# Two metaformer layers on one core: small VectorE work moved to GpSimd, one fetch per tile for the small Mamba, new durations and places in the planner

## The chip, the cores and the metric

The kernel runs on one core of a Trainium2 chip. The metric is the device time of one execution in microseconds (us). A core has TensorE (PE, with its weight loads PEld), VectorE (DVE), ScalarE (ACT), GpSimd (POOL) and SyncE (SP), each with its own list of instructions that it works off in order, and 16 DMA engines. Nearly all DMAs are issued by SP, the indirect ones (gathers and scatters of rows) by POOL.

## The reference

The input `x` is 8 images of 256 channels and 32 x 32 positions (1024 tokens). Two layers follow each other. In short:

```python
# layer 0
x = x + mamba0(ln_c(x))            # 512 inner channels, 16 states, 1024 steps in time:
                                   # h = exp(dt*A)*h + dt*xs*B ;  y = sum_s h*C + xs*D ; y*silu(z)
t = tokens(x)
t = t + moe(ln_t(t))               # 8 experts, top 2 of the softmax of the gate, gelu, hidden 512
# layer 1
x = x + conv1(ln_c(x))             # channels 0..127 kept; 3x3, 1x11 and 11x1 depthwise taps on 32 each;
                                   # a small mamba on the last 32 (64 inner channels, 16 states)
t = t + mod(ln_t(t))               # the best 511 of 1024 tokens pass a 256-1024-256 feed forward
```

`dt` is `softplus(...)`. Both Mambas are first-order recurrences along the tokens, one for each channel and state.

## The kernel before

The work is cut into 16 units (image, half of the 1024 tokens; `N = 512`) for the large Mamba, and 4 groups of two images for all that follows. A unit holds 512 channels as four tiles of 128; `scan_unit` goes over them in two couples `cp`, over the 16 states in 8 steps `sp` of two states `j`, and over the two tiles `n` of the couple. Each innermost step is one `scan_pair`:

- GpSimd multiplies `dtx` by a row of B for both states (L780, 128 x 1024, tile `dbu`),
- ScalarE makes `exp(dt*A)` into PSUM (L785), VectorE scans it with `dbu` (L788, `tensor_tensor_scan`) and multiplies by a row of C (L793), for each of the two states,
- TensorE adds the two products into `y` with an identity matrix (L804); where `paired` says so, GpSimd adds the two first (L797) and TensorE adds one. `PAIRED` gives, for each of the 16 units and the 4 small Mambas, in how many of 8 steps that is so.

The rows of B and C lie in DRAM (`rows`) and are spread over the partitions by DMA into tiles `bc` of 128 x 2 x 512 f32 (512 KB, four of them). The large Mamba fetches one tile by one DMA (L839, source `[128 (stride 0), 2 x 512]`), and two scan pairs share a couple of tiles. The small Mamba (`mamba_scan`, one for each group) has two images on the partitions, 64 each, whose rows differ, so a tile is fetched by two DMAs of 64 partitions (L1416), and each scan pair needs tiles of its own: 16 pairs and 32 tiles in each of the four scans.

`delta` makes `dt` (softplus as max(v, 0) + ln(1 + exp(-|v|))): TensorE product, ScalarE abs, exp and ln, VectorE max and sum (L758), and GpSimd's product `dtx = dt * xs` (L760). `small_rstd` makes `rstd` on ScalarE and `shift = -mean * rstd` on VectorE (L859), for tokens (128 x 4) and in `combine` (128 x 2). `gate` in `tokens` makes the gate's logits with four small VectorE operations (L914 to L917).

After four units, a group passes `route` (ranks of experts, VectorE), `scatter` (rows to their experts' slots), `experts` (23 blocks of 256 rows, weights fetched for each), `combine` (rows of the two experts of a token gathered by POOL, weighted and summed by TensorE with diagonal matrices `wdiag`, L1254 to L1263, evicted by ScalarE, L1267), `taps_of` (the convolutions on VectorE, L1323), `mamba_in`, `mamba_scan`, `mamba_out`, `assemble`, `ranks`, `feed_forward` and `finish`.

No engine's order is written by hand. Every step is declared with an engine, an estimated duration, a priority, and what it reads and writes; `Flow.run` is a list scheduler at build time that plays the steps against these estimates and emits them in the order in which it would start them. `PLAN` and `UNIT_AT` give the priorities ("places") of the stages; `dma` estimates a transfer at 2.3 us + KB / 180 behind its issue. Idle TensorE time in the plan is filled with dummy products (L525, L529). The estimates do not run on the chip: they decide only the order of each engine's list.

Of the kernel before, what the change touches and what calls it, by code (L numbers as in the profile page):

```python
# [30 lines left out]
AF = mybir.ActivationFunctionType  # L31
# [24 lines left out]

PAIRED = [2, 4, 0, 4, 3, 4, 7, 5, 5, 6, 8, 7, 5, 8, 6, 6, 7, 7, 5, 6]

# [3 lines left out]
PLAN = [  # L62
    dict(put=10.59, experts=(180, 8.0), combine=(355, 4.88), taps=(436, 2.05), mamba=464, assemble=(486, 1.12), ranks=500, ffn=(521, 4.8), finish=(570, 2.4)),
    dict(put=6.24, experts=(357, 6.25), combine=(465, 1.5), taps=(550, 0.75), mamba=541, assemble=(568, 2.41), ranks=628, ffn=(722, 4.8), finish=(767, 3.75)),
    dict(put=5.3, experts=(465, 5), combine=(602, 2.94), taps=(701, 1.84), mamba=666, assemble=(681, 1.88), ranks=699, ffn=(791, 2.81), finish=(827, 2.89)),
    dict(put=2.65, experts=(603, 4), combine=(692, 0.86), taps=(761, 0.77), mamba=775, assemble=(796, 0.43), ranks=795, ffn=(836, 3), finish=(873, 3.07)),
]
# [28 lines left out]
ENGINES = (PE, ACT, DVE, POOL, SP)  # L96
HOP = 0.08
SWITCH = 1.3
PACE = 1.07
AHEAD = 100  # L100
# [72 lines left out]
class Flow:  # L173
# [29 lines left out]
    def dma(self, prio, kb, run, reads=(), writes=(), fills=(), claims=(), us=0.4):  # L203
        return self.step(SP, us, prio, run, reads, writes, fills, claims, lat=2.3 + kb / 180)

    def run(self):
# [17 lines left out]
        def earliest(s):  # L224
            at = now[s.engine]
            for d in s.needs:
                at = max(at, d.end + (HOP if d.engine != s.engine or d.lat else 0.0))
            taken = {}
            for b in s.fresh:
                if b.v is None:  # L230
                    k = taken[b.pool] = taken.get(b.pool, 0) + 1
                    if not b.pool.has(k, b):
                        return None
                    at = max(at, sorted(b.pool.free)[k - 1][0] + HOP)
            if s.engine == SP and len(flying) >= QUEUE:
                at = max(at, sorted(flying)[-QUEUE])
            return at
# [61 lines left out]
def layers(g, ctx, x, a, out):  # L299
# [446 lines left out]

    def delta(parts, dts, dtxs, xs, prio):

        v, l = banks(2), buf("sq")
        for n in range(2):  # L750
            left, right, made = parts[n]
            step(PE, 0.9, prio, lambda n=n, left=left, right=right: nc.tensor.matmul(
                v[n].v, left, right(), start=True, stop=True), [made], [v[n]], claims=[*v, l, dts])
            step(ACT, 0.6, prio + 0.5, lambda n=n: nc.scalar.activation(l.v[:, n * N : (n + 1) * N], v[n].v, AF.Abs), [v[n]], fills=[l])
        step(ACT, 1.1, prio + 1, lambda: nc.scalar.activation(l.v, l.v, AF.Exp, scale=-1.0), [], [l], table="exp")
        step(ACT, 1.15, prio + 1, lambda: nc.scalar.activation(l.v, l.v, AF.Ln, bias=g.one), [], [l], table="exp")
        for n in range(2):
            step(DVE, 0.72, prio + 1.5, lambda n=n: nc.vector.scalar_tensor_tensor(  # L758
                dts.v[:, n], v[n].v, 0.0, l.v[:, n * N : (n + 1) * N], ALU.max, ALU.add), [v[n], l], fills=[dts])
        gpsimd(2.4, prio + 2, lambda: nc.gpsimd.tensor_tensor(dtxs.v, dts.v, xs.v, ALU.mult), [dts, xs], [dtxs])  # L760

    def dt_of(i, cp, prio):
        u = units[i]
        dts, dtxs = u[f"dt{cp}"], u[f"dtx{cp}"] = buf(f"dt{cp}"), buf(f"dtx{cp}")
        dbl = u["dbl"]
        parts = [
            (w_dt[: DR0 + 1, c * P : (c + 1) * P], lambda: dbl.v[: DR0 + 1], dbl) for c in (2 * cp, 2 * cp + 1)
        ]
        delta(parts, dts, dtxs, u[f"xs{cp}"], prio)

# [83 lines left out]
    def small_rstd(mv, rstd, shift, eps, prio, made, fill):  # L854

        step(ACT, 0.5, prio, lambda: (
            nc.scalar.activation(rstd(), mv()[:, :, 1:2], AF.Ln, bias=eps),
            nc.scalar.activation(rstd(), rstd(), AF.Exp, scale=-0.5)), made, fills=fill[:1], table="exp")
        return step(DVE, 0.6, prio, lambda: nc.vector.scalar_tensor_tensor(  # L859
            shift(), mv()[:, :, 0:1], -1.0, rstd(), ALU.mult, ALU.mult), [*made, fill[0]], fills=fill[1:])  # L860

    def tokens(i, prio):
# [47 lines left out]
        def gate():  # L910

            lg = grp["logits"].v[:, blks]
            wide = [P, nb, E]
            nc.vector.tensor_tensor(raw.v, raw.v, grp["rstd"].v[:, blks].to_broadcast(wide), ALU.mult)  # L914
            nc.vector.tensor_tensor(lg, gsum.to_broadcast(wide), grp["shift"].v[:, blks].to_broadcast(wide), ALU.mult)
            nc.vector.tensor_tensor(lg, lg, raw.v, ALU.add)
            nc.vector.tensor_tensor(lg, lg, gate_b.unsqueeze(1).to_broadcast(wide), ALU.add)  # L917

        step(DVE, 1.6, now, gate, [grp["rstd"], grp["shift"]], [raw], [grp["logits"]])

    def route(n, prio):
# [120 lines left out]
        for part in range(8):  # L1044
            step(DVE, 1.7, prio + 1 + 0.25 * part, lambda part=part: better(part), [lg], [r])
        step(DVE, 0.6, prio + 3, masks, [], [r])
        step(PE, 0.5, prio + 3, counts, [r], [pt])
        step(DVE, 1.0, prio + 3.5, sums, [pt], [r])
        step(DVE, 0.8, prio + 4, ends, [], [r])
# [8 lines left out]
    def put(kind, dest, slots, index, src, grp, prio, name, sources):  # L1058
# [20 lines left out]

        step(POOL, 1.15, prio, run, sources, fills=[slots], lat=2.5)  # L1080

# [148 lines left out]
    def combine(n, prio, each):  # L1230
# [6 lines left out]
        for m in range(NI):  # L1237
# [5 lines left out]
                xc.v, grp["gx"].v[:, at : at + 2]), [grp["gx"], grp["y"]], [xc], claims=[at_a, at_b]).opens = line  # L1243
            (t,), xo = banks(), buf("xo")
            for h in range(2):
                blk = i * NI + j + h
                ys, ds = buf("ys", line), buf("wdiag", line)
                for q in range(2):
# [3 lines left out]
                        in_offset=bass.IndirectOffsetOnAxis(ap=idx.v[:, blk : blk + 1], axis=0)),  # L1252
                        [grp["y"], idx], fills=[ys], lat=2.5)
                    step(ACT, 0.4, now - 1, lambda q=q, ds=ds, wt=wt, blk=blk: nc.scalar.activation(  # L1254
                        ds.v[:, q], g.ident, AF.Copy, scale=wt.v[:, blk]), [wt], fills=[ds])

                def product(h=h, blk=blk, ys=ys, ds=ds, xc=xc, t=t):
                    rows = slice(32 * (blk // 4), 32 * (blk // 4) + 32)
                    at = t.v[:, h * C : (h + 1) * C]
                    nc.tensor.matmul(at, g.ident, xc.v[:, h], start=True, stop=False)  # L1260
                    for q in range(2):
                        nc.tensor.matmul(at, ds.v[:, q], ys.v[:, q], start=False, stop=False)  # L1262
                    nc.tensor.matmul(at, grp["cwt"].v[rows], b2[rows, blk % 4], start=False, stop=True)  # L1263

                step(PE, 1.9, now, product, [ys, ds, xc, grp["cwt"]], [t], claims=[xo])
            bn = buf("bn")
            step(ACT, 0.6, now + 0.3, lambda xo=xo, t=t: nc.scalar.copy(  # L1267
                xo.v, t.v.rearrange("p (h c) -> p h c", h=2)), [t], [xo])
            dma(now + 0.5, 256, lambda xo=xo, two=two, i=i: nc.sync.dma_start(x1.v[:, two, i], xo.v), [xo], fills=[x1])
# [134 lines left out]
    def mamba_scan(n, pos):  # L1404
# [3 lines left out]
        for sp in range(DS // 2):  # L1408
            for hf in range(2):
                both = buf("bc"), buf("bc")  # L1410
                for j in range(2):

                    def fetch(j=j, hf=hf, sp=sp, both=both):
                        for i in range(2):
                            at = i * 2 * DS + j * DS + 2 * sp
                            nc.sync.dma_start(  # L1416
                                both[j].v[i * DI1 : (i + 1) * DI1],
                                grp["rows"][hf].v[at : at + 2].partition_broadcast(DI1),
                            )

                    dma(pos + 2 * sp + hf - 6, 512, fetch, [grp["rows"][hf]], [both[j]], us=0.8)
                scan_pair(
# [22 lines left out]
    def assemble(n, prio, each):  # L1445
# [8 lines left out]
        for j in range(NI):  # L1454
# [33 lines left out]

            step(DVE, 1.9, now + 0.7, stats, [xc], [bn, junk], [tok])

# [117 lines left out]
    def finish(n, prio, each):  # L1608
# [3 lines left out]
        for m in range(NI):  # L1612
# [6 lines left out]
            for h in range(2):  # L1619
# [3 lines left out]
                    in_offset=bass.IndirectOffsetOnAxis(ap=slot.v[:, 1, at : at + 1], axis=0)),  # L1623
                    [grp["y2"][i], slot], fills=[ys], lat=2.5)
                step(ACT, 0.59, now - 1, lambda h=h, at=at, xc=xc: nc.scalar.activation(
# [14 lines left out]

            step(DVE, 1.3, now, added, [tok, ys], [xc])
            step(PE, 0.7, now + 0.2, turned, [xc], [t], claims=[xo])
# [195 lines left out]
```

## Time and profile before

| | us |
|---|---|
| three runs, median (lowest to highest) | 3852.95 (3839.76 to 3853.16) |
| the profiled execution: time | 3870.05 |
| the profiled execution: span from first to last instruction | 3868.2 |
| large Mamba's scans, first to last (L788) | 58 to 2995 |
| small Mambas' scans of groups 2 and 3 | 3279 to 3386, 3558 to 3652 |
| busy: PE / DVE / ACT / POOL | 3299 / 2978 / 2207 / 2328 |

The profile is of one execution. Busy times are sums of instruction durations on an engine; a wait is idle time of an engine together with what ended it. A busy PE includes the dummy products. A line number names a line of the kernel. Lines such as `L1416 SPq DMA_DIRECT2D bc<-rows` are DMA issues: SP hands the transfer over and goes on, and the transfer lands later.

### The profile page before, as it was taken

The numbers are of one execution on the slowest core, as the hardware profiler recorded it, in microseconds if no ns is written. First come the engines' busy times: TensorE is split into PE (matmuls) and PEld (weight loads), VectorE is DVE, ScalarE is ACT, GpSimd is POOL, SyncE is SP. The second block draws the span as 40 slices with busy tenths as digits, with TensorE's granted clock in tenths as the row PEclk, the third lists the DMA queues.
The fourth block names the chain that finished last, engine by engine and source line by source line (L and its number), as shares of the span: only waits on it lengthen the run. The fifth ranks groups of instructions, "written<-read, shape, count | busy, mean of one in ns | idle before, by whom it ended". The sixth has DMA issues, their size and how long they took to land. (4 is left out here: it accounts for less than half of the span.)

```text
span 3868.2 us, 38209 instructions
## 1 busy us (share of the span) xinstructions
PE 3299.0 (85%) x10818; PEld 1849.4 (48%) x10818; DVE 2978.3 (77%) x4281; ACT 2207.2 (57%) x4010; POOL 2327.8 (60%) x1587
## 2 busy tenths in 40 slices
PE   8888888788889888978997798988987889799768
PEld 3333333333544444434553444554555666566446
DVE  4899899989679978976898898779787527557751
ACT  4555565465757557645765665665764456556433
POOL 3567567588577768866775886545765433424522
PEclk9999999999999999998999999999888989899989
DMA  6333333344544435535553558654669666967955
GB/s 232 122 123 131 114 131 132 106 151 162 200 139 167 165 129 194 181 111 172 172 174 122 195 181 226 204 184 136 200 204 223 222 213 214 243 215 215 247 175 168
DMA packets 277073, 676.67 MB, mean 175 GB/s; under 512 B 33063, under 2 KB 114349, under 8 KB 276862
## 3 DMA queue, kind: packets, MB, share of 16 engines
q1 hardware_dynamic: 258430, 623.88, 51.2%
q0 software_dynamic: 18432, 50.36, 4.1%
q8 instruction: 87, 1.43, 0.2%
q14 instruction: 124, 1.02, 0.1%
HBM read 572.92 MB, written 101.19 MB: 174 GB/s over the span
## 5 line engine op out<-in xcount | busy, mean ns | idle before, releaser
L780 POOL TENSOR_TENSOR dbu<-dtx,bc 128x1024 f32<-128x1024 f32 x576 | 1359.3, 2368 | 515.6 <-PE y L804 349.0
L804 PE MATMUL y<-dbu,ident 128*128 128x512 f32 x1564 | 822.6, 635 | 217.9 <-POOL dbu L797 185.7
L785 ACT ACTIVATE mm<-dt,neg_a 128x512 f32<-128x512 f32 x1152 | 770.3, 688 | 208.2 <-DVE dbu L793 190.4
L788 DVE TENSOR_TENSOR_SCAN mm<-mm,dbu 128x512 f32<-128x512 f32 x576 | 703.9, 1222 | 229.7 <-ACT mm L785 153.8
L793 DVE TENSOR_TENSOR dbu<-mm,bc 128x512 f32<-128x512 f32 x1152 | 796.4, 691 | 81.4 <-DMA bc<-rows 18.0
L788 DVE TENSOR_TENSOR_SCAN mm<-mm,state,dbu 128x512 f32<-128x512 f32 x576 | 738.2, 1282 | 59.5 <-POOL dbu L780 38.7
L797 POOL TENSOR_TENSOR dbu<-dbu 128x512 f32<-128x512 f32 x370 | 480.9, 1301 | 299.4 <-DVE dbu L793 291.3
L804 PEld LDWEIGHTS y<-dbu,ident 128*128 128x128 f32 x1564 | 281.6, 197 | 560.5 <-POOL dbu L797 278.7
L1179 PE MATMUL mm<-we,hid 128*128 128x256 f32 x1984 | 486.4, 398 | 36.0 <-ACT state L792 13.0
L792 ACT COPY state<-mm 128x1 f32<-128x1 f32 x576 | 91.4, 160 | 731.6 <-DVE dbu L793 710.9
L1157 PE MATMUL mm<-xbt,we 128*128 128x256 f32 x1984 | 474.3, 391 | 30.4 <-DMA we<-in_W12f 10.4
L1179 PEld LDWEIGHTS mm<-we,hid 128*128 128x128 f32 x1984 | 387.8, 199 | 156.3 <-issue 47.4
L1157 PEld LDWEIGHTS mm<-xbt,we 128*128 128x128 f32 x1984 | 383.4, 196 | 139.2 <-issue 46.9
L525 PE MATMUL y<-still 128*128 128x512 bf16 x1059 | 275.7, 395 | 0.0
L721 PE MATMUL mm<-pre,w_tap 128*128 128x512 f32 (+3 forms) x512 | 240.8, 612 | 28.6 <-ACT pre L708 27.3
L440 ACT ACT_TABLE_LOAD x176 | 225.8, 1283 | 3.1
L1250 POOL DMA_INDIRECT ys<-slots_y,slot x128 | 122.2, 954 | 160.0 <-PE mm L1262 69.0
L1163 ACT ACTIVATE hid<-mm,we 128x256 f32<-128x256 f32 x496 | 196.8, 475 | 37.8 <-PE mm L1157 29.1
L525 PEld LDWEIGHTS <-still 128*128 128x128 bf16 x1059 | 105.9, 101 | 192.6 <-issue 118.8
L721 PEld LDWEIGHTS mm<-pre,w_tap 128*128 128x128 f32 x512 | 95.5, 193 | 166.8 <-issue 103.9
L1068 POOL DMA_INDIRECT slots_x<-xg,slot x128 | 129.8, 1014 | 68.4 <-DVE acc_b L1323 31.2
L1621 POOL DMA_INDIRECT ys<-y,slot_t x64 | 63.1, 986 | 158.7 <-DVE xc L1631 59.0
(251 smaller groups left out, 3983.6 us busy)
## 6 DMA issues: line engine op xcount, KB each, us to landing
bc<-rows SPq DMA_DIRECT2D x512, 512.0 KB
bc<-rows SPq DMA_DIRECT2D x256, 256.0 KB
we<-in_W SPq DMA_DIRECT2D x92, 514.0 KB
we<-in_W SPq DMA_DIRECT2D x92, 512.0 KB
xb<-slots_x SPq DMA_DIRECT2D x92, 256.0 KB
slots_y<-xo SPq DMA_DIRECT2D x92, 256.0 KB
we<-in_W12f SPq DMA_DIRECT2D x32, 514.0 KB
xc<-x SPq DMA_DIRECT2D x64, 256.0 KB
```

Of the source, the lines that this page charges most:

```text
L440: nc.scalar.preload_act_table_set(tables[name])
L525: nc.tensor.matmul(live[0].v[:, 0], still, wide, start=False, stop=False)
L721: nc.tensor.matmul(tc_.v[:, cut:], w_tap[:, c, j], pre.v[:, cut + j : j + N], start=j == 3, stop=j == 0)
L780: gpsimd(2.45, prio, lambda: nc.gpsimd.tensor_tensor(dbu.v, dtxs.v[:, n : n + 1].to_broadcast(wide2), bt.v, ALU.mult), [dtxs, bt], [dbu], ...
L785: step(ACT, 0.69, prio, lambda j=j, h=h: nc.scalar.activation(h.v, dts.v[:, n], AF.Exp, scale=scales(j)), [dts], [h], table="exp", scan=True)
L788: step(DVE, 1.25, prio, lambda j=j, h=h: nc.vector.tensor_tensor_scan(h.v, h.v, dbu.v[:, j], 0.0 if initial is None else initial[1](j), AL ...
L793: step(DVE, 0.68, prio, lambda j=j, h=h: nc.vector.tensor_tensor(dbu.v[:, j], h.v, ct.v[:, j], ALU.mult), [h, ct], [dbu], scan=True)
L797: gpsimd(1.3, prio + 2.3, lambda: nc.gpsimd.tensor_tensor(dbu.v[:, 0], dbu.v[:, 0], dbu.v[:, 1], ALU.add), [], [dbu])
L804: nc.tensor.matmul(y.v[:, n], g.ident, dbu.v[:, j], start=False, stop=stop and (paired or j == 1))
L1157: nc.tensor.matmul(tv[:, f], we[0].v[:, at : at + P], xbt.v[:, k], start=k == 0, stop=k == KC - 1)
L1163: nc.scalar.activation(hid.v[:, f], tv[:, f % 2], func, bias=we[0].v[:, at : at + 1])
L1179: nc.tensor.matmul(to, hid.v[:, f, h * P : (h + 1) * P], we[1].v[:, f * C : (f + 1) * C], start=extra is None and f == 0, stop=f == FC - 1,)
```

## The change

The change does the following.

- `mamba_scan`: one DMA for each tile instead of two. Its source is a view of `rows` as `[2, 64 (stride 0), 2, 512]`, its destination the whole tile of 128 partitions.
- `delta`: except for unit 0, ScalarE writes `relu(v)` into `dts` (two instructions), and GpSimd adds `ln(1 + exp(-|v|))` (128 x 1024); VectorE's two operations are left out there.
- `small_rstd` and `gate`: the VectorE operations become GpSimd operations (two for `shift`, four for the gate).
- `combine` of groups 2 and 3: TensorE makes only the bias product (L1263); VectorE weights and adds the two experts' rows (two operations on each of two blocks) and adds `xc`; no `wdiag`, no eviction by ScalarE.
- `PAIRED`: 348 sums on GpSimd instead of 370, the others on TensorE.
- Planner: DMA estimate 3.4 us + KB / 250, indirect DMAs 3.0 to 3.3 us instead of 2.5, a `DRAIN` of 0.15 us behind TensorE, `PACE` 1.05 instead of 1.07, some step durations, and new places in `PLAN`.

The diff, cut to its core:

```diff
-PAIRED = [2, 4, 0, 4, 3, 4, 7, 5, 5, 6, 8, 7, 5, 8, 6, 6, 7, 7, 5, 6]
+PAIRED = [2, 2, 0, 4, 0, 5, 8, 5, 5, 7, 8, 8, 5, 5, 6, 5, 7, 7, 5, 5]
 PLAN = [
-    dict(put=10.59, experts=(180, 8.0), combine=(355, 4.88), taps=(436, 2.05), mamba=464, assemble=(486, 1.12), ranks=500, ffn=(521, 4.8), finish=(570, 2.4)),
-    dict(put=6.24, experts=(357, 6.25), combine=(465, 1.5), taps=(550, 0.75), mamba=541, assemble=(568, 2.41), ranks=628, ffn=(722, 4.8), finish=(767, 3.75)),
-    dict(put=5.3, experts=(465, 5), combine=(602, 2.94), taps=(701, 1.84), mamba=666, assemble=(681, 1.88), ranks=699, ffn=(791, 2.81), finish=(827, 2.89)),
-    dict(put=2.65, experts=(603, 4), combine=(692, 0.86), taps=(761, 0.77), mamba=775, assemble=(796, 0.43), ranks=795, ffn=(836, 3), finish=(873, 3.07)),
+    dict(put=2.64, experts=(180, 8.0), combine=(358, 2.93), taps=(451, 3.28), mamba=464, assemble=(496, 1.12), ranks=500, ffn=(521, 4.8), finish=(613, 2.21)),
+    dict(put=9.37, experts=(357, 6.25), combine=(505, 1.88), taps=(545, 1.2), mamba=551, assemble=(563, 2.41), ranks=630, ffn=(745, 3.84), finish=(768, 2.81)),
+    dict(put=5.28, experts=(465, 5), combine=(562, 2.94), taps=(659, 4.42), mamba=643, assemble=(684, 1.5), ranks=685, ffn=(791, 1.69), finish=(797, 4.62)),
+    dict(put=2.65, experts=(603, 4), combine=(692, 0.33), taps=(755, 1.54), mamba=775, assemble=(776, 0.43), ranks=753, ffn=(812, 3), finish=(841, 3.07)),
 ]
...
-        return self.step(SP, us, prio, run, reads, writes, fills, claims, lat=2.3 + kb / 180)
+        return self.step(SP, us, prio, run, reads, writes, fills, claims, lat=3.4 + kb / 250)
...
             step(ACT, 0.6, prio + 0.5, lambda n=n: nc.scalar.activation(l.v[:, n * N : (n + 1) * N], v[n].v, AF.Abs), [v[n]], fills=[l])
+            if not soon:
+                step(ACT, 0.6, prio + 0.6, lambda n=n: nc.scalar.activation(dts.v[:, n], v[n].v, AF.Relu), [v[n]], fills=[dts])
...
+        if soon:
+            for n in range(2):
+                step(DVE, 0.72, prio + 1.5, lambda n=n: nc.vector.scalar_tensor_tensor(
+                    dts.v[:, n], v[n].v, 0.0, l.v[:, n * N : (n + 1) * N], ALU.max, ALU.add), [v[n], l], fills=[dts])
+        else:
+            gpsimd(2.4, prio + 1.5, lambda: nc.gpsimd.tensor_tensor(
+                dts.v.rearrange("p n t -> p (n t)"), dts.v.rearrange("p n t -> p (n t)"), l.v, ALU.add), [l], [dts])
...
-        return step(DVE, 0.6, prio, lambda: nc.vector.scalar_tensor_tensor(
-            shift(), mv()[:, :, 0:1], -1.0, rstd(), ALU.mult, ALU.mult), [*made, fill[0]], fills=fill[1:])
+        def product():
+            nc.gpsimd.tensor_tensor(shift(), mv()[:, :, 0:1], rstd(), ALU.mult)
+            nc.gpsimd.tensor_scalar(shift(), shift(), -1.0, None, ALU.mult)
+
+        gpsimd(0.3, prio, product, [*made, fill[0]], fills=fill[1:])
...
-        step(DVE, 1.6, now, gate, [grp["rstd"], grp["shift"]], [raw], [grp["logits"]])
+        gpsimd(0.8, now, gate, [grp["rstd"], grp["shift"]], [raw], [grp["logits"]])
...
+            late = n >= 2
...
+                def weighted(h=h, blk=blk, ys=ys, xo=xo, t=t):
+                    nc.vector.scalar_tensor_tensor(
+                        xo.v[:, h], ys.v[:, 0], grp["weight0"].v[:, blk], t.v[:, h * C : (h + 1) * C], ALU.mult, ALU.add
+                    )
+                    nc.vector.scalar_tensor_tensor(
+                        xo.v[:, h], ys.v[:, 1], grp["weight1"].v[:, blk], xo.v[:, h], ALU.mult, ALU.add
+                    )
...
+            if late:
+                step(DVE, 0.9, now + 0.3, lambda xo=xo, xc=xc: nc.vector.tensor_tensor(
+                    xo.v, xo.v, xc.v, ALU.add), [xc], [xo])
...
                     def fetch(j=j, hf=hf, sp=sp, both=both):
-                        for i in range(2):
-                            at = i * 2 * DS + j * DS + 2 * sp
-                            nc.sync.dma_start(
-                                both[j].v[i * DI1 : (i + 1) * DI1],
-                                grp["rows"][hf].v[at : at + 2].partition_broadcast(DI1),
-                            )
-
-                    dma(pos + 2 * sp + hf - 6, 512, fetch, [grp["rows"][hf]], [both[j]], us=0.8)
+
+                        rows = grp["rows"][hf].v.rearrange("(i m) n -> i m n", i=2)
+                        at = j * DS + 2 * sp
+                        nc.sync.dma_start(
+                            both[j].v, rows[:, at : at + 2].unsqueeze(1).to_broadcast([2, DI1, 2, N]))
+
+                    dma(pos + 2 * sp + hf - 6, 512, fetch, [grp["rows"][hf]], [both[j]])
```

## The prediction

> **What bounds the kernel now.** I read the page first, then the busy time by stretch, then who waits for whom, then single lines. The stretches are cut where the fetches of the small Mamba (L1416) begin and end. Columns: stretch, length, busy us and count of PE, PEld, DVE, ACT and POOL, granted clock, DMA share, GB/s.
>
> ```profile
> 150.00:900.00 750.00, 641.40 (x1713) 271.99 (x1712) 690.21 (x854) 406.44 (x709) 503.49 (x292) 0.96 0.38 129
> ...
> 2329.00:2436.00 107.00, 89.03 (x272) 46.69 (x270) 84.22 (x102) 61.88 (x104) 67.15 (x42) 0.95 0.83 210
> ...
> 2857.00:2991.00 134.00, 109.28 (x377) 72.86 (x375) 98.29 (x120) 68.69 (x123) 70.73 (x40) 0.86 0.87 221
> ...
> 3264.00:3385.00 121.00, 92.49 (x342) 64.93 (x341) 63.15 (x67) 72.33 (x124) 55.95 (x33) 0.89 1.01 250
> ...
> 3536.00:3648.00 112.00, 82.80 (x311) 50.35 (x310) 90.11 (x85) 66.93 (x119) 73.61 (x47) 0.92 0.98 263
> ```
>
> In the large scans (first row) VectorE is busy 690 of 750 us: a pair of states costs it two scans of 1.22 us and two products of 0.69 us, 3.82 us, and ScalarE mostly waits for it. The other four rows are the four scans of the small Mamba. There the 16 DMA engines are full (0.83 to 1.01) and VectorE is not. These 474 us are DMA-bound stretches in a kernel that is otherwise bound by VectorE (scans) and TensorE (experts). The fetches themselves, and who waited for them:
>
> ```profile
> L1416 SPq DMA_DIRECT2D bc<-rows x256: 444/498/995, 2328.9 to 3642.3; - x128
> ...
>   POOL dbu L780: 115.8, 35
> ```
>
> The reader sees 256 issues, two for each of 128 tiles (four scans, 8 steps, 2 halves, 2 tiles), and GpSimd starved for 116 us by them. A tile is 128 rows of 4 KB, 0.524 MB; a scan takes 32 of them, 16.8 MB. The packet records give a 4 KB packet a median of 159 ns in 150 to 900 us, but 284 ns at 3290 to 3380 us: the half-tile fetches run at little over half speed.
>
> **What the Trainium skill says.** "SBUF — State Buffer", Door 1: 64 partitions reach only half of the memory's DMA ports, 128 all of them. The 284 against 159 ns agree. So one fetch over 128 partitions looks like a gain. But "DMA: Bandwidth & Descriptors", Why a DMA increments its semaphore by 16 and not by 1, says that a transfer from SP runs on k engines, the largest k up to 16 that divides the slowest dimension (not of size 1) of both access patterns, and that each engine used writes one completion. The trace of before can be held against that:
>
> ```profile
> DMA packets 277073, 676.67 MB, mean 175 GB/s; under 512 B 33063, under 2 KB 114349, under 8 KB 276862
> ```
>
> There are 1,597 transfers on SP's queue and 384 on POOL's. With 16 completions each that is 31,696 packets, and the loads with rows under 512 B add 1,408 by their shapes: 33,104. The page has 33,063, 41 fewer. Three transfers have an outer size that is no multiple of 16: W_dt with 17 rows (k = 1, 15 fewer), w_dt1 with 5 (k = 5, 11 fewer), fb2 with one (k = 1, 15 fewer): 41 exactly. The rule holds in this program. The new fetch reads `[2, 64, 2, 512]`: its outermost dimension is 2, so k = 2. The same page's Rules for kernel authors warns of just such an outermost dimension. No transfer of before is of this kind, so its speed isn't shown.
>
> **The change, part by part.** *The fetch.* Out go 256 issues of 0.498 us on SP, in come 128: 64 us less of SP's queue, worth nothing where SP waits for buffers. By k = 2 a tile is 64 packets on each of two engines, always the same two by the page. At 159 ns (no port is crowded by two engines) that is 10.2 us a tile, 20.4 us a pair of states, where VectorE needs 3.82. A scan: 32 x 10.2 = 326 us. The two engines also carry a sixteenth of all else: the rows above moved 22.5, 29.6, 30.2 and 29.5 MB, less 16.8 each leaves 5.7, 12.8, 13.4, 12.7 MB; a sixteenth at 4096 B in 159 ns is 14, 31, 32, 31 us. The stretches become 340, 357, 358, 357 = 1,412 us against 474: **+938 us**. Nothing covers it. Each engine runs its list in order, and the pairs stand among the experts' and other scans' instructions: behind a GpSimd product that waits for its tile stand further pairs and indirect DMAs; TensorE's sums wait for it with expert products behind them; SP, which waits for one of the four bc tiles to come free, holds up weights and stores. Weights once issued queue behind up to four tiles, 41 us, on those two engines. Bounds: with the 150-to-900 average, 129 GB/s at share 0.38, an engine makes 21.2 GB/s and a tile 12.4 us, 70 us more a scan, +280. Below, the new order may lay more other work into these stretches than before's; I allow half of the excess hidden at most, -440. I take +938.
>
> *Small work off VectorE.* The rstd/shift product (L859) and the gate's four operations (L914 to L917) go to GpSimd; for all but two of 36 calls the softplus sum does too.
>
> ```profile
> L859 DVE SCALAR_TENSOR_TENSOR rs<-mv,rs x32: 151/164/8916, 1775.7 to 3499.7; 128x2 f32<-128x2 f32 x32
> L859 DVE SCALAR_TENSOR_TENSOR shift<-mv,rstd x16: 151/1240/7552, 232.9 to 2945.0; 128x4 f32<-128x4 f32 x16
> ```
>
> An operation of 0.15 us takes up to 8.9. "SBUF — State Buffer", Who interferes with whom: a VectorE instruction with two SBUF inputs waits for a GpSimd instruction that reads SBUF, here products of 2.4 us; the trace agrees, since the scan's own operations, with one input in PSUM, are never stretched so. Removed: 16 x 1.768 + 32 x 1.229 = 67.6; gate 16 x (0.179 + 0.725 + 0.322 + 0.446) = 26.8; softplus 68 x 0.683 = 46.4: 141 us of VectorE, about 135 of it before 2991. Added to GpSimd: 34 x 2.37 = 81, 96 small ones at L711's 0.188 = 18, 64 gate operations at about 0.22 (an estimate from the same row) = 14; less pairs are summed there (348 for 370, 22 x 1.30 = 29 off, and 22 TensorE products of 0.635 on): net +84 on an engine 67% busy in the first row. Added to ScalarE: 68 relus at L754's 0.598 = 41. The dt path gets longer: relu 0.6 and sum 2.37 for 0.68, +2.3 us, 34 times, ahead of dtx, behind which the next scan's products stand on GpSimd: +78 if all is exposed. Gain between -135 (VectorE always last) and +78 - 40 = +38. VectorE ends most waits but idles a tenth: I take 60% of 135, **-80**.
>
> *Late experts' rows.* For groups 2 and 3 TensorE loses 64 x 0.410 + 32 x 0.424 = 40 us, ScalarE 64 x 0.395 + 16 x 0.588 = 35; VectorE gains 64 x 0.58 (L1631, same shape) + 16 x 0.69 = 48, in stretches where it is half idle. The sums of a tile of rows, 2.3 us and 0.7, follow the rows' arrival, as products and eviction did: -10, between -40 and +30.
>
> *New durations and places.* They run nowhere on the chip; they only order the lists. From 2857 on TensorE idles 172 us, which bounds a gain; a worse order could cost 60. I take -10.
>
> **Sum.** 938 - 80 - 10 - 10 = +838. The profiled execution took 3870.05 us (span 3868.2), the median shown is 3852.95, 17 below. 3870 + 838 - 17 = 4691: **4690 us**.
>
> **Rivals.** *All 16 engines.* If the fetch is split by partitions after all, because the instruction carries another pattern than the source writes, the port crowding goes: 16.8 MB at 129/0.38 = 339 GB/s take 50 us and the rest 17 to 40, so a stretch falls to 80 or 90 us, above VectorE's 61 for 16 pairs: about 30 saved in each, of which half reaches the end: -60; with -100 for the other parts 3870 - 160 - 17 = 3693, say 3620 to 3790. For it: the crowded packets and the 116 us of starved GpSimd. Against it: the 41 missing completions. It decides at k: from k = 8 on (16 packets, 2.5 us a tile) a pair's two tiles take 5.1 us, less than the 6.7 us that a pair takes in the shortest of the four stretches, and the fetch is no loss. *GpSimd sets the pace.* With a neutral fetch and the dt path exposed, +38 and nothing from the places: 3870 + 38 - 17 = 3891. Against it: GpSimd's idle third. *Nothing to see:* gains and the longer path cancel, 3840 to 3870.
>
> **How the numbers follow.** Two engines 0.80; GpSimd's pace 0.03; nothing to see 0.03; all engines 0.14. Faster means over 0.5% (19 us), about what a measurement of this kernel can tell from no change. Slower 0.83, same 0.03, faster 0.14. The likeliest case alone spans 4250 (half hidden) to 5000 (12.4 us a tile); that holds nearly all of its 0.80, so it is also the range.
>
> **What would show it.** Right: 128 issues at the fetch's line; GpSimd's products waiting for DMA bc<-rows over 800 us in total; four stretches of some 350 us where the DMA share is low, since fourteen engines rest, with tiles 20 us a pair; under 512 B fewer packets, by 256 x 16 - 128 x 2 = 3,840. VectorE's tiny L859 gone, its scan stretches above 0.92 busy. Wrong: completions fewer by only 2,048 and a DMA share in these stretches under 0.8 at over 250 GB/s; then the all-engines case holds.

## The result, and the profile after

The change made the kernel slower: 4790.45 us (median of 4 runs, 4782.17 to 4807.18) against 3846.84 us (4 runs, 3839.76 to 3853.16), a ratio of 1.2459, 95% interval 1.2412 to 1.2506. The profiled execution took 4807.18 us (span 4805.5). In the changed kernel the lines move down a little: the product `dbu` is L787 instead of L780, the scan L795 instead of L788, the product with C L800 instead of L793, the fetch of the small Mamba L1448 instead of L1416, the `shift` product L868 instead of L859.

The same busy time by stretch, now of the changed kernel; the last four rows are its four scans of the small Mamba. Columns: stretch, length, busy us and count of PE, PEld, DVE, ACT and POOL, granted clock, DMA share, GB/s.

```profile
150.00:900.00 750.00, 656.14 (x1752) 291.21 (x1751) 654.92 (x804) 418.54 (x744) 509.02 (x324) 0.95 0.40 137
2331.00:2650.00 319.00, 126.66 (x311) 66.91 (x310) 78.04 (x93) 64.28 (x106) 59.48 (x45) 0.67 0.18 68
3096.00:3463.00 367.00, 145.44 (x470) 99.59 (x469) 111.46 (x178) 83.15 (x145) 73.30 (x58) 0.67 0.27 92
3656.00:4011.00 355.00, 113.39 (x334) 74.39 (x332) 81.56 (x78) 73.05 (x125) 59.14 (x34) 0.66 0.24 83
4220.00:4567.00 347.00, 107.46 (x306) 61.32 (x305) 72.66 (x77) 59.59 (x106) 61.20 (x39) 0.63 0.21 76
```

The four stretches grew from 474 to 1,388 us, and every compute engine is idle most of the time in them. The DMA share is the telling column. Before, it was 0.83 to 1.01: all 16 DMA engines were nearly full. Now it is 0.18 to 0.27, and the kernel still waits for transfers. That points to few engines that carry the load, which the experiments test. The fetch, those who waited for it, and the packet count of the changed kernel:

```profile
L1448 SPq DMA_DIRECT2D bc<-rows x128: 482/2910/11363, 2331.3 to 4560.8; - x128
...
  POOL dbu L787: 1001.9, 57
...
  DVE dbu L800: 450.2, 60
```

```profile
DMA packets 273232, 676.64 MB, mean 141 GB/s; under 512 B 29223, under 2 KB 110509, under 8 KB 273022
```

There are 128 issues instead of 256, and GpSimd waits 1,002 us for these tiles instead of 116. The packets under 512 B, most of them the completions that a transfer writes, are 3,840 fewer (33,063 - 29,223), which is 256 x 16 - 128 x 2: each of the new transfers writes two completions instead of 16. The packet records show it a second way: from the first to the last issue of the first scan, exactly two packets of 4 KB are in flight for 88% of the time.

### The profile page after: what moved, and what is told of

The parts are those of the page before. It is cut to its first block, busy times and chain, and to the rows that moved or that the text cites. A ratio compares the mean times of both kernels' runs of the same rounds, so it can differ in the third digit from the quotient of the medians.

```text
span 4805.5 us, 37890 instructions
## 1 busy us (share of the span) xinstructions
PE 3395.5 (71%) x10732; PEld 1896.3 (39%) x10732; DVE 2902.4 (60%) x4181; ACT 2203.4 (46%) x3995; POOL 2413.2 (50%) x1772
## 2 busy tenths in 40 slices
DMA packets 273232, 676.64 MB, mean 141 GB/s; under 512 B 29223, under 2 KB 110509, under 8 KB 273022
## 5 line engine op out<-in xcount | busy, mean ns | idle before, releaser
L787 POOL TENSOR_TENSOR dbu<-dtx,bc 128x1024 f32<-128x1024 f32 x576 | 1361.3, 2371 | 1427.7 <-DMA bc<-rows 1007.2
L811 PE MATMUL y<-dbu,ident 128*128 128x512 f32 x1608 | 876.6, 657 | 551.1 <-POOL dbu L804 443.9
L800 DVE TENSOR_TENSOR dbu<-mm,bc 128x512 f32<-128x512 f32 x1152 | 796.4, 691 | 511.5 <-DMA bc<-rows 450.9
L795 DVE TENSOR_TENSOR_SCAN mm<-mm,dbu 128x512 f32<-128x512 f32 x576 | 704.5, 1223 | 533.9 <-POOL dbu L787 321.7
L795 DVE TENSOR_TENSOR_SCAN mm<-mm,state,dbu 128x512 f32<-128x512 f32 x576 | 738.4, 1282 | 364.3 <-POOL dbu L787 307.5
L1168 PE MATMUL mm<-xbt,we 128*128 128x256 f32 x1984 | 501.0, 406 | 254.2 <-DMA we<-in_W 144.5
L811 PEld LDWEIGHTS y<-dbu,ident 128*128 128x128 f32 x1608 | 301.6, 204 | 914.5 <-POOL dbu L804 581.0
L804 POOL TENSOR_TENSOR dbu<-dbu 128x512 f32<-128x512 f32 x348 | 449.9, 1294 | 271.8 <-DVE dbu L800 263.4
L1190 PE MATMUL mm<-we,hid 128*128 128x256 f32 x1984 | 511.3, 413 | 89.8 <-DMA we<-in_W 33.4
L1168 PEld LDWEIGHTS mm<-xbt,we 128*128 128x128 f32 x1984 | 401.7, 205 | 372.0 <-issue 203.0
L1190 PEld LDWEIGHTS mm<-we,hid 128*128 128x128 f32 x1984 | 405.2, 208 | 214.0 <-issue 70.5
L526 PE MATMUL y<-still 128*128 128x512 bf16 x1097 | 296.3, 407 | 0.0
L1263 POOL DMA_INDIRECT ys<-slots_y,slot x128 | 125.9, 984 | 145.2 <-DMA xc<-gx 62.1
L1153 PE MATMUL mm<-ident,xb 128*128 128x128 f32 x432 | 75.0, 302 | 166.8 <-ACT state L799 77.1
L893 PE MATMUL mm<-w_out,sz 128*128 128x264 f32 x512 | 136.8, 414 | 52.4 <-ACT state L799 29.7
```

What stands on the lines that cost most here:

```text
L526: nc.tensor.matmul(live[0].v[:, 0], still, wide, start=False, stop=False)
L787: gpsimd(2.45, prio, lambda: nc.gpsimd.tensor_tensor(dbu.v, dtxs.v[:, n : n + 1].to_broadcast(wide2), bt.v, ALU.mult), [dtxs, bt], [dbu], ...
L795: step(DVE, 1.25, prio, lambda j=j, h=h: nc.vector.tensor_tensor_scan(h.v, h.v, dbu.v[:, j], 0.0 if initial is None else initial[1](j), AL ...
L800: step(DVE, 0.68, prio, lambda j=j, h=h: nc.vector.tensor_tensor(dbu.v[:, j], h.v, ct.v[:, j], ALU.mult), [h, ct], [dbu], scan=True)
L804: gpsimd(1.3, prio + 2.3, lambda: nc.gpsimd.tensor_tensor(dbu.v[:, 0], dbu.v[:, 0], dbu.v[:, 1], ALU.add), [], [dbu])
L811: nc.tensor.matmul(y.v[:, n], g.ident, dbu.v[:, j], start=False, stop=stop and (paired or j == 1))
```

## The experiments

Ratios are to the kernel before, run beside each experiment, with 95% intervals. The median of the kernel before lay between 3845 and 3862 us in the different groups of experiments, so kernels are compared by ratio. The theory is the prediction's: the new fetch runs on two DMA engines, and the rest is worth a few per cent at most. The rivals: the changed order does the damage, or the moved operations do.

**Only the fetch.** The kernel before, with the changed kernel's single transfer:

```diff
-                        for i in range(2):
-                            at = i * 2 * DS + j * DS + 2 * sp
-                            nc.sync.dma_start(
-                                both[j].v[i * DI1 : (i + 1) * DI1],
-                                grp["rows"][hf].v[at : at + 2].partition_broadcast(DI1),
-                            )
+                        rows = grp["rows"][hf].v.rearrange("(i m) n -> i m n", i=2)
+                        at = j * DS + 2 * sp
+                        nc.sync.dma_start(
+                            both[j].v, rows[:, at : at + 2].unsqueeze(1).to_broadcast([2, DI1, 2, N]))
```

> The kernel before with nothing changed but the small Mamba's fetch: one transfer with source [2, 64 (stride 0), 2, 512]; the order of every engine's list stays that of before. Theory 'two engines': the four stretches of the fetches grow from 475 us together to 1360 to 1420, so 4740 to 4790 us in all, and the packets under 512 B fall by 3840. Rival 'the rest' (new places, longer path of dt): the fetch alone costs nothing or saves up to 100 us, 3750 to 3860.

Measured: 4837.0 us, ratio 1.2595 (1.2563 to 1.2628). Its first and second small scan in the busy time by stretch, columns as above:

```profile
2328.00:2646.00 318.00, 122.66 (x271) 59.53 (x269) 79.90 (x97) 60.15 (x98) 59.98 (x39) 0.66 0.18 66
3092.00:3443.00 351.00, 133.15 (x376) 85.56 (x375) 93.20 (x120) 70.14 (x127) 69.57 (x39) 0.65 0.23 83
```

With the old order and the old work on every engine, the rows look as in the changed kernel. A single 4 KB packet is not slow in these stretches (median 162 ns, 264 to 279 ns before), but only two are in flight at a time, for 88% of the first scan. The fetch alone costs a little more than the whole change, and more than the 4740 to 4790 us that were expected; the section on the prediction says where the rest lies.

**Everything but the fetch.** The reverse edit in the changed kernel: all else stays, the two transfers of 64 partitions come back.

> The changed kernel with the fetch alone put back to two transfers of 64 partitions; the order of every list stays that of the changed kernel. Theory 'two engines': 3790 to 3890 us, the stretches back at 100 to 135 us each; what is left against before is all other edits together, which the prediction put at -100 and the profiles (937 in all less 911 in the stretches) at about +26. Rival 'the rest': 4600 or more, since the loss lies in the other edits.

Measured: 3804.61 us, ratio 0.989 (0.9861 to 0.9919), 40 us below before. The product of the two ratios, 1.2595 x 0.989 = 1.2456, is the ratio of the whole change, so within these intervals the two parts don't disturb each other.

**How the cost goes with the number of engines.** If the count k follows the outermost dimension of the source, 4 and 8 there must give a series. Sizes and bytes of the transfers stay; the groups of partitions get rows of B and C that are not those that the Mamba needs, so these two kernels serve for the time alone. The lines that take the place of the two transfers in the kernel before:

```diff
+                        rows = grp["rows"][hf].v.rearrange("(i m) n -> i m n", i=4)   # second kernel: i=8
+                        at = (j * DS + 2 * sp) % 16                                   # % 8
+                        nc.sync.dma_start(
+                            both[j].v, rows[:, at : at + 2].unsqueeze(1).to_broadcast([4, P // 4, 2, N]))   # [8, P // 8, 2, N]
```

> The kernel before, in its own order, with one fetch whose source is [4, 32 (stride 0), 2, 512]: the four quarters of the partitions read four different pairs of rows, so the small Mamba is given wrong rows of B and C; sizes and bytes are as in the changed kernel. Theory 'two engines' as a law of the outermost size: four engines, 32 packets each, 5.1 us a tile, 163 us a scan; with 10 to 30 us of other traffic the stretches are 175 to 195 us, packets under 512 B are 33063 - 4096 + 512 = 29479, and the whole takes 4080 to 4150 us. Rival (the stride-0 read of two sources costs a fixed time a tile): stretches as with two, 320 to 350 us.

> As the last, with [8, 16 (stride 0), 2, 512]: eight engines, 16 packets, 2.5 us a tile, 81 us a scan. Stretches 90 to 115 us, packets under 512 B 33063 - 4096 + 1024 = 29991, and 3800 to 3860 us in all, about as before. Rival: stretches of 320 us or more.

Measured: 4208.91 us, ratio 1.0939 (1.0886 to 1.0991), and 3966.46 us, ratio 1.0308 (1.0256 to 1.0361). First small scan of each in the busy time by stretch, outermost dimension 4, then 8:

```profile
2333.00:2509.00 176.00, 106.94 (x270) 52.90 (x267) 80.53 (x98) 59.87 (x98) 62.60 (x40) 0.78 0.34 121
```

```profile
2331.00:2452.00 121.00, 97.27 (x270) 50.60 (x267) 85.00 (x101) 61.45 (x103) 63.28 (x41) 0.89 0.59 183
```

The packet counts of the two pages are 29,479 and 29,991: 256 and 768 above the 29,223 of two engines, which is 128 x 2 and 128 x 6, so k was 4 and 8. The packets in flight agree: in the first scan exactly four of 4 KB for 75% of the time, and exactly eight for 55%. The mean length of the four stretches falls from 343 us (k = 2, the fetch alone) to 196 and 143, longer than expected in both, as are the whole times. With eight engines, eight or more packets (completions left out) are in flight for 93 to 96% of each of the four stretches. That fits eight engines that have hardly any time to spare.

**All 16 engines with one transfer.** The outermost dimension of the source must be the partitions. That is so when the images alternate from partition to partition instead of lying in two halves, since then the address repeats every second partition:

```diff
-                            both[j].v, rows[:, at : at + 2].unsqueeze(1).to_broadcast([2, DI1, 2, N]))
+                            both[j].v, rows[:, at : at + 2].unsqueeze(0).to_broadcast([DI1, 2, 2, N]))
...
+    def mixed(v, axis):
+        return np.stack(np.split(v, 2, axis), axis + 1).reshape(v.shape)
...
-        "w_xm": twice(c1["in_proj_w"][:DI1].T),
+        "w_xm": mixed(twice(c1["in_proj_w"][:DI1].T), 1),
```

and in the same way for the other six constants of the small Mamba. It was tried in the changed kernel and in the kernel before.

> The changed kernel with the two images interleaved on the partitions of the small Mamba's inner channels (the weights' columns and rows are stored in that order), so that one fetch reads [64 (stride 0), 2, 2, 512]: still one transfer over 128 partitions, but with an outermost dimension of 64. Theory 'two engines': k is 16 again and no port is crowded, the stretches fall to 75 to 100 us, 3750 to 3850 us in all, and packets under 512 B are 2048 fewer than before (31015). Rival 'form' (a single fetch that reads two sources by a stride of 0 is slow whatever its outermost size): 4750 or more, as the changed kernel.

> The kernel before, in its own order, with the interleaved channels and the single fetch [64 (stride 0), 2, 2, 512]. Theory 'two engines': the stretches fall from 107 to 135 us each by 20 to 35 us, and 50 to 120 us of it reach the end: 3730 to 3800 us. Rival 'form': 4740 or more. A third answer, 3840 to 3860, would say that the crowded ports of the two fetches cost nothing at the end.

Measured: in the changed kernel 3756.5 us, ratio 0.9761 (0.9727 to 0.9795), faster than the kernel before and than the changed one; in the kernel before 3798.37 us, ratio 0.9875 (0.9847 to 0.9903). The four small scans of the first of these:

```profile
2328.00:2433.00 105.00, 95.84 (x313) 54.31 (x311) 81.74 (x96) 67.54 (x111) 65.00 (x46) 0.98 0.71 229
2843.00:2988.00 145.00, 122.27 (x478) 88.35 (x477) 127.56 (x175) 83.30 (x146) 74.95 (x58) 0.92 0.71 243
3158.00:3257.00 99.00, 85.87 (x333) 59.34 (x331) 81.53 (x78) 72.99 (x126) 63.73 (x35) 0.97 0.87 304
3448.00:3544.00 96.00, 83.06 (x309) 50.04 (x310) 77.08 (x79) 58.42 (x105) 68.63 (x43) 0.94 0.85 283
```

The packets under 512 B are 31,015 in both, 2,048 fewer than before, or 128 x 16: one transfer for each tile, on 16 engines. A single transfer that repeats two sources is thus not slow by itself; the outermost dimension decides. The DMA share is below full, although the four stretches take 444 us together, against 488 with the two transfers in the same order. Of the waiting for the tiles (columns: waiter, awaited, us in total, times, longest) this is left:

```profile
POOL dbu L787 <- DMA bc<-rows: 62.9, 34, 6.0
```

With the two transfers in the same order it was 130.0 us. A 4 KB packet in these stretches takes a median of 159 ns, as in the large scans; in the kernel before it took 264 to 279 ns. That agrees with the Trainium skill, "SBUF — State Buffer", Door 1, by which a transfer of 64 partitions reaches only half of the memory's ports.

**The other parts, one at a time, in the kernel before.** First the small VectorE operations of `small_rstd` and `gate`, moved to GpSimd as in the change; then its softplus (relu on ScalarE, sum on GpSimd); then the weighted rows of the late experts; then only `PAIRED`, `PLAN`, `DRAIN`, `PACE`, the DMA estimate and the step durations. The core of the first two:

```diff
-        return step(DVE, 0.6, prio, lambda: nc.vector.scalar_tensor_tensor(
-            shift(), mv()[:, :, 0:1], -1.0, rstd(), ALU.mult, ALU.mult), [*made, fill[0]], fills=fill[1:])
+        def product():
+            nc.gpsimd.tensor_tensor(shift(), mv()[:, :, 0:1], rstd(), ALU.mult)
+            nc.gpsimd.tensor_scalar(shift(), shift(), -1.0, None, ALU.mult)
```

```diff
+                step(ACT, 0.6, prio + 0.6, lambda n=n: nc.scalar.activation(dts.v[:, n], v[n].v, AF.Relu), [v[n]], fills=[dts])
...
+            gpsimd(2.4, prio + 1.5, lambda: nc.gpsimd.tensor_tensor(
+                dts.v.rearrange("p n t -> p (n t)"), dts.v.rearrange("p n t -> p (n t)"), l.v, ALU.add), [l], [dts])
```

> The kernel before with small_rstd's product and the gate's four operations on GpSimd, nothing else; old durations and places. Theory A (what VectorE loses is filled with other waits because the lists are ordered by the planner and ScalarE's exp or GpSimd's products end last next): within 15 us of before, 3830 to 3860, with VectorE's busy time down by 60 to 95 us and its idle time up by as much. Theory B (VectorE sets the pace and the longer dt path of the softplus edit eats the gain): 40 to 70 us faster, 3775 to 3805. Theory C (the new places cost in the scans what the offload gains): as B for this run.

> The kernel before with the softplus' second half on ScalarE (relu) and GpSimd (sum), nothing else. Theory A: within 15 us of before. Theory B: 20 to 60 us slower, with GpSimd's product dtx late and ScalarE's exp behind it. Theory C: 20 to 30 us faster, since 46 us of VectorE go.

> The kernel before with groups 2 and 3 weighting the experts' rows on VectorE (and the gather's estimate in that loop at 3.3 us), nothing else. All theories: nothing in the scans; the end 0 to 30 us earlier by the 40 us of TensorE and 35 us of ScalarE that go in the last 900 us. If the 40 us that the changed kernel with two fetches gains comes from here, 3800 to 3815.

> The kernel before with the new durations, places and PAIRED alone; no operation moves to another engine. If the 40 us come from the places: 3795 to 3815. Theory C: the first fetch of the small Mamba comes 20 us or more later than at 2329 us. Theory A: the first fetch within 10 us of 2329.

Measured:

| part alone | median, us | ratio to before |
|---|---|---|
| small operations | 3844.03 | 0.9975 (0.9963 to 0.9988) |
| softplus | 3893.90 | 1.0122 (1.0093 to 1.0150) |
| late experts' rows | 3848.68 | 0.9997 (0.9979 to 1.0014) |
| durations, places, `PAIRED` | 3849.70 | 1.0002 (0.9986 to 1.0018) |

Of the three theories in the expectations, A fits the small operations and B the softplus; neither fits both. The places alone cost and gain nothing at the end, but they bring the first fetch 20 us later (2349 instead of 2329 us), which is the sign of theory C; the rest of the kernel makes up for it. The softplus part alone is a loss. From 150 to 2329 us, VectorE's waits in the kernel before, then with the small operations moved, then with the softplus moved (there the scan is L794 and the product L786):

```profile
DVE mm L788 <- ACT mm L785: 129.1, 75, 9.4
...
DVE mm L788 <- POOL dbu L780: 18.5, 6, 11.4
```

```profile
DVE mm L788 <- ACT mm L785: 137.0, 83, 8.1
DVE mm L788 <- POOL dbu L780: 41.2, 12, 9.2
```

```profile
DVE mm L794 <- ACT mm L791: 134.6, 71, 9.2
DVE mm L794 <- POOL dbu L786: 65.7, 19, 14.0
```

VectorE's busy time in that stretch fell by 53 us (1,893.9 to 1,840.6) and 49 us (to 1,844.6), yet the first fetch of the small Mamba came at 2334 and 2372 us instead of 2329. The wait for GpSimd's product grew from 18.5 to 41.2 and 65.7 us. With the softplus on GpSimd the scans lost 43 us before the first fetch, and that is the whole loss; behind it nothing was lost. The wait for GpSimd is not all of it: up to its own first fetch VectorE was busy only 8 us less, although 54 softplus operations of 36.8 us had gone. Six more operations of the convolutions' taps (12 us) stood ahead of the fetch, and other operations took more or less time than before: the gate's four 26 us more, those of L859 20 us less. So the planner's order has a part in the 43 us.

**Whether the parts need each other.** The four parts sum to some 30 us of loss alone, and gain 40 together. So two parts were undone, one in each run, in the fastest kernel, the changed one with the interleaved fetch: the softplus goes back to VectorE, or the old durations, places and `PAIRED` come back.

> The changed kernel with the interleaved channels (one fetch on 16 engines) and with the softplus' second half back on VectorE; new places, durations and PAIRED kept. If the softplus edit costs what it cost alone (47 us) under any plan: 3700 to 3720 us, faster than the 3756 of the interleaved changed kernel. If the new PAIRED and durations take its cost in (28 us less of pair sums on GpSimd, lists ordered with the right durations): 3745 to 3775.

> The changed kernel with the interleaved channels and all moved operations, but with the old durations, places and PAIRED. If the effects of the parts add up (small -8, softplus +42 to +47, late experts -3, each measured alone): 34 us above the old kernel with the same fetch (3798), so 3820 to 3850, and the new plan is worth 65 to 95 us once the operations are moved, though it was worth nothing without them. If the parts gain together under any plan: 3740 to 3775, as with the new one.

Measured: without the softplus move 3780.42 us, ratio 0.9794 (0.9769 to 0.9819); with the old plan 3822.0 us, ratio 0.9888 (0.9863 to 0.9912). The plan, worth nothing alone, is worth 1.3% in the kernel with the operations moved (0.9888 against 0.9761); the plan alone was tried with two transfers only. The softplus move, a loss of 1.2% alone, costs nothing under the new plan: 0.9761 with it, 0.9794 without, intervals that overlap. And under the old plan the moved operations together make no difference (0.9888 against 0.9875 of the kernel before with the interleaved fetch). By its raw time the run with the old plan lies where a sum of the parts had put it (3820 to 3850 us), but the kernel before was slower beside it, and by the ratios the sum would be 0.997. So the softplus' 43 us do not belong to the move as such: with the small operations moved as well, under the same old plan, the first fetch comes at 2332 us.

## Why the prediction was right, and where it was not

Right were the sign, the mechanism and nearly the size: 4690 foretold, 4790 measured, inside the range and in the likeliest case. The parts that it put at -100 together were -40. Its steps one by one:

- **Two engines.** Confirmed. The completions missing (3,840) were those of k = 2 to the packet, k = 4 and 8 gave their own counts, and the packets in flight were two, four and eight. This is the rule of the Trainium skill, "DMA: Bandwidth & Descriptors", Why a DMA increments its semaphore by 16 and not by 1; the trace agrees.
- **+938 for the fetch.** The fetch alone cost 992 us by the medians and 957 in the profiled executions. The stretches were foretold as 1,412 us against 474; from the first issue to 6 us after the last they were 1,373 (fetch alone) and 1,386 (whole change) against 475. What the sum left out lies behind them: the last tile lands late. From the last issue to the product with the finished sum (L821) it took 48, 31, 33 and 35 us with the new fetch alone, 18, 17, 17 and 15 before: +80. So the stretches were estimated too long, and the tails behind them not at all; that the total came so near is in part because the two errors cancel. Stretches and tails together make 977 of the 992 us: hardly any of the loss was hidden under other work.
- **-100 for all else.** It was -40. The mis-sized term is **-80 for the small work off VectorE**: it took 60% of VectorE's saved time as saved. The nearest measurement is the pair with the interleaved fetch and the old plan, without and with the moved operations. From 150 to 2329 us, first without, then with the moved operations, the busy time by engine (columns as above) and VectorE's waits:

```profile
150.00:2329.00 2179.00, 1876.48 (x5554) 937.50 (x5553) 1890.75 (x2326) 1287.71 (x2264) 1524.34 (x939) 0.95 0.46 152
```

```profile
DVE mm L788 <- ACT mm L785: 127.5, 73, 9.5
...
DVE mm L788 <- POOL dbu L780: 19.8, 7, 11.4
```

```profile
150.00:2329.00 2179.00, 1870.44 (x5527) 943.80 (x5526) 1829.39 (x2208) 1290.95 (x2305) 1608.82 (x1064) 0.94 0.46 152
```

```profile
DVE mm L794 <- ACT mm L791: 175.5, 94, 8.8
...
DVE mm L794 <- POOL dbu L786: 26.5, 19, 6.0
```

VectorE is busy 61 us less (1,890.8 to 1,829.4), but the first fetch comes at 2332 us instead of 2333, and the kernel ends no sooner (0.9888 against 0.9875). All the saved time became idle time, most of it in front of a scan that waits for ScalarE's exp. The stretched small operations were real: all 24 calls of L859 that took over 0.3 us in the kernel before ended within 0.04 us of the end of a GpSimd operation that they overlapped. But without them VectorE only waited for something else. With the softplus alone GpSimd's product ended more of the waits, with all operations moved ScalarE's exp; the longer dt path, priced at up to +78 in the GpSimd rival, may have a part in both, which is not shown.

- **-10 each for the late experts' rows and for the places.** Alone both are 0. For the rows the prediction counted one record to a TensorE product, where the trace holds two (half of the 256 records of L1262 and half of the 128 of L1260 went), so 63 us of busy time left TensorE instead of 40, and still nothing came of it at the end. The places, worth nothing alone, are worth 1.3% together with the moved operations. That gain lies late in the kernel: with the interleaved fetch and the moved operations, the time from the first fetch to the end is 1,490 us under the old plan and 1,429 under the new one, while the first fetch comes at 2332 and 2328 us. The prediction had put most of its -100 in the large scans.
- **The all-engines rival** was wrong for this instruction. When the interleaved fetch makes all 16 engines work, the changed kernel takes 3756.5 us, inside the rival's range (3620 to 3790) but above its 3693: its 80 to 90 us a stretch were 96 to 145, and its -100 for the other parts has the same fault as above.
- **"From k = 8 on the fetch is no loss"** was wrong: +3.1%. A tile was priced at 16 packets of 159 ns alone. The eight engines also carry a part of the other traffic, and the 4 KB packets of the four stretches took a median of 165 to 219 ns, a tenth of them over 304 to 334 ns; eight or more packets were in flight nearly all the time. What slows these packets isn't settled.
- **What would show it.** All marks came about as stated but one: VectorE in the scan stretch is not above 0.92 busy but at 654.92 / 750 = 0.87. Taking work off it made it idle, not faster; this was the sign that the -80 failed.

Open: how the new places and the moved operations help each other, and why ScalarE's exp ends later when operations move. All edits but those of the fetch alone make the planner order every list anew. The new places by themselves moved the first fetch by 20 us, so differences of that size between these kernels cannot be put down to one moved operation.

## What to carry to other kernels

Before two transfers are joined into one, look at the outermost dimension of the new source pattern: here 2, 4, 8 and 64 in that place gave 2, 4, 8 and 16 DMA engines, and a layout that puts the partitions there kept all 16. A low DMA share beside long waits for a DMA was the mark of few engines here, not of spare capacity. Taking work off the busiest engine pays only as far as its neighbours can feed it sooner; ask which waits stand next to it first, and plan the order anew together with the move.

## What the runs showed of the hardware beyond that

The clock that TensorE was granted fell where it was starved: 0.63 to 0.67 in the changed kernel's four small scans against 0.86 to 0.95 before, with a mean over the span of 0.847 against 0.940. It returned with the work: 0.78 and 0.89 in the first scan with four and eight engines, 0.98 with the interleaved fetch. With it the TensorE work in a stalled stretch got longer: the 40 sums of L804 in the first scan took a mean of 637 ns each in the kernel before and 861 ns with the new fetch alone, which leaves them as they are.
